# Copying position weights ahead of the transposes: one ScalarE copy, or four GpSimd copies by groups

## The chip, the cores and the metric

The kernel runs on one core of a Trainium2 chip. The metric is the device time of one execution in microseconds; lower is better. A core has five engines that run their own instruction streams: TensorE (PE in the profile, its weight loads PEld), VectorE (DVE), ScalarE (ACT), GpSimd (POOL) and SyncE (SP), which here only issues DMAs. Each engine takes its instructions in order; they wait for each other through semaphores.

## The reference

Two layers act on x of shape (2, 512, 64, 64) in float32. Layer 0, where the change lies, is a deformable convolution: for each pixel and each of 16 channel groups it predicts nine sampling offsets and a softmax mask, samples the projected image bilinearly, and projects the sum.

```python
xproj = inp @ in_w + in_b
x1 = gelu(layernorm(depthwise_conv3x3(x) + dw_b))
offset = x1 @ off_w + off_b
mask = softmax((x1 @ mask_w + mask_b).reshape(N, H, W, G, P), -1)
out = _dcnv3_core(xproj, offset, mask)   # 9 bilinear samples a group
out = out @ out_w + out_b
...
x = x + _L0(_gn(x), ...)                 # layer 0, group norm ahead
x = x + _L1(_gn(x), ...)                 # layer 1: attention over 4096 pixels, batch norm
```

## The kernel before

**Layer 0** takes about the first third of the time. The two images are cut into 16 chunks of 512 pixels (eight rows of 64), and each chunk passes four stages, all of them generators whose steps are interleaved by hand:

- project (line 758): normalise the rows on ScalarE (xn), multiply by in_w on TensorE (pq), copy out (xj, line 764) and store the image as pixel rows (xt) in HBM.
- features (from line 771): a 3x3 depthwise convolution as nine taps per channel block. The first is on ScalarE; eight are scalar_tensor_tensor on VectorE (line 788), each reading two SBUF tensors. GpSimd adds the blocks (tot, lines 794 and 796) for the layer norm's mean; Gelu follows.
- weights (from line 833): TensorE multiplies the features by the offset and mask weights (po, line 842), VectorE adds the bias (o, line 847). Since all offsets here are smaller than one pixel, the nine bilinear samples fall in a 5x5 window, so the stage builds, for each pixel and group, 25 position weights: aw of 128 pixels x 5 x 5 x 64, where the 64 are four pixel blocks times 16 groups. GpSimd clears aw (line 838), VectorE adds nine 3x3 products to it (lines 885 and 890). Then aw is rearranged into at, laid out as group, block, position (padded from 25 to 32); TensorE transposes it, four groups into one PSUM tile p_tr (line 901), and ScalarE copies each tile to awT (line 902).
- sample (from line 919): TensorE spreads awT over the pixels of small patches (pb, line 930), ScalarE copies that to bt (line 935), TensorE multiplies it with the image patches (pa, line 949), ScalarE copies to dT (line 961), TensorE applies out_w (py, line 970), and VectorE adds bias and x and takes statistics (lines 975 and 976).

The order on every engine is written out in the function period. In one period, sample works on chunk i, weights on chunk i+1, features and project further ahead. The copy from aw to at is the last step of weights within a period; its four transposes are the first steps of the next one. On ScalarE's queue the copies xj and dT of other stages stand behind it. In the first image's periods the statistics of the second image (pieces xraw, line 713) are slipped between VectorE's steps (image_stats).

The PSUM tiles pq, p_tr, po, py and the means share one tag with four buffers; at shares a buffer with tx of the same stage; aw has one buffer, so the next clearing of aw waits until the copy has read it.

**Layer 1** (from line 1112 on) is the attention. It touches nothing of the change.

Of the kernel before, what the change touches and what calls it, by code (L numbers as in the profile page):

```python
# [523 lines left out]
NW = 25  # L524
# [46 lines left out]
def window_path(ctx: ExitStack, tc: tile.TileContext, t_in: dict, out: bass.AP, far: bass.AP, sums: bass.AP):  # L571
    nc = tc.nc
# [57 lines left out]
    with ExitStack() as l0:  # L630
# [66 lines left out]
        def image_stats(n):  # L697

            mv = sm.tile([P, KB, 2], F32, name="gn_mv")
            size = CH if n == 0 else CH // 2  # L700
            pieces, ahead = deque((kb, h) for kb in range(KB) for h in range(S // size)), deque()
            for kb in range(KB):
                st = sm.tile([P, 16, 6], F32, name="gn_st")
                for h in range(S // size):
                    if n == 0:
                        t = img[kb][:, h * size : (h + 1) * size]
                    else:
                        while len(ahead) < 3 and pieces:
                            k2, h2 = pieces.popleft()
                            ahead.append(io.tile([P, size], F32, name="xraw", bufs=3))  # L710
                            nc.sync.dma_start(ahead[-1], x_v[n, :, k2, h2 * size : (h2 + 1) * size])
                        t = ahead.popleft()
                    nc.vector.bn_stats(st[:, h, :], t)
                    yield
                nc.vector.bn_aggr(mv[:, kb, :], st[:, : S // size].rearrange("p a b -> p (a b)"))
            yield
            result = []
            yield from group_norm_steps(mv, KB, sm, ps, result)
            sc, bi = result
            gn[n] = [sm.tile([P, KB], F32, name=f"gn_{k}{n}") for k in ("scale", "bias")]  # L720
            nc.vector.tensor_copy(gn[n][0], sc)
            nc.vector.tensor_copy(gn[n][1], bi)
# [110 lines left out]
        def weights(i):  # L833

            f = feats.pop(i)
            o = sm.tile([P, 3, NP, 4 * G], F32, name="o")
            aw = sm.tile([P, 5, 5, 4 * G], F32, name="aw")
            nc.gpsimd.memset(aw.rearrange("p y x q -> p (y x q)"), 0.0)
            for t in range(4):
                po = ps.tile([P, CH], F32, tag="mm", name="po")  # L840
                for kb in range(KB):
                    nc.tensor.matmul(  # L842
                        po[:, : 3 * GP], f[:, kb, t * P : (t + 1) * P], om_w[:, kb].rearrange("p a k g -> p (a k g)"),
                        start=(kb == 0), stop=(kb == KB - 1),
                    )
                yield
                nc.vector.tensor_add(
                    o[:, :, :, t * G : (t + 1) * G].rearrange("p a k g -> p (a k) g"),
                    po[:, : 3 * GP].rearrange("p (a g) -> p a g", g=G), om_b.rearrange("p a k g -> p (a k) g"),
                )  # L850
                yield

            m = o[:, 2]
            nc.scalar.activation(m, m, AF.Exp)
            yield

            tx = sm.tile([P, 2, 3, NP, 4 * G], F32, tag="tx", name="tx")
            for d, by in ((0, -1.0), (2, 1.0)):
                nc.vector.tensor_scalar(tx[:, :, d], o[:, 0:2], by, 0.0, ALU.mult, ALU.max)
            nc.vector.scalar_tensor_tensor(  # L860
                tx[:, :, 1].rearrange("p a k q -> p a (k q)"), tx[:, :, 0].rearrange("p a k q -> p a (k q)"), 1.0,
                tx[:, :, 2].rearrange("p a k q -> p a (k q)"), ALU.subtract, ALU.subtract, reverse0=True
            )
            yield

            nc.scalar.activation(o[:, 0:2], tx[:, :, 1], AF.Relu, scale=-1.0, accum_out=far[:, i : i + 1])
            yield
            sx = sm.tile([P, 4 * G], F32, name="sx")
            nc.vector.tensor_reduce(sx, m.rearrange("p k q -> p q k"), AX.X, ALU.add)
            rs = sm.tile([P, 4 * G], F32, name="rs")  # L870
            nc.vector.reciprocal(rs, sx)
            nc.gpsimd.tensor_add(sums[:, 0], sums[:, 0], sx)
            nc.gpsimd.tensor_add(sums[:, 1], sums[:, 1], rs)
            nc.vector.tensor_mul(m, m, rs.unsqueeze(1).to_broadcast([P, NP, 4 * G]))
            yield
            my = sm.tile([P, 3, NP, 4 * G], F32, name="my")
            nc.vector.tensor_mul(my, tx[:, 1], m.unsqueeze(1).to_broadcast([P, 3, NP, 4 * G]))
            yield
            myk = my.rearrange("p d k q -> p k d q")
            txk = tx[:, 0].rearrange("p d k q -> p k d q")  # L880
            for k in (4, 0, 1, 2, 3, 5, 6, 7, 8):
                kx, ky = divmod(k, 3)
                dst = aw[:, ky : ky + 3, kx : kx + 3, :]
                pk = dst if k == 4 else sm.tile([P, 3, 3, 4 * G], F32, tag="pk", name="pk")
                nc.vector.tensor_mul(  # L885
                    pk, myk[:, k].unsqueeze(2).to_broadcast([P, 3, 3, 4 * G]),
                    txk[:, k].unsqueeze(1).to_broadcast([P, 3, 3, 4 * G]),
                )
                if k != 4:
                    nc.vector.tensor_add(dst, dst, pk)  # L890
                yield
            at = sm.tile([P, G, 4, 32], F32, tag="tx", name="at")
            nc.scalar.copy(
                at.rearrange("p g t w -> p w t g")[:, :NW], aw.rearrange("p y x (t g) -> p (y x) t g", t=4)
            )
            yield

            for b in range(4):
                pt = ps.tile([P, 4, P], F32, tag="mm", name="p_tr")
                for g in range(4):  # L900
                    nc.tensor.transpose(pt[:, g, :], at[:, 4 * b + g].rearrange("p t w -> p (t w)"), ident)
                nc.scalar.copy(awT[:, 4 * b : 4 * b + 4, :], pt)  # L902
                yield
# [186 lines left out]

        run(image_stats(0), project(0), value_weights(), features(0), project(1))
        v = Chain(weights, 0)
        v(23)
        run(features(1), project(2), output_bias())
        fetch(0, 0)
        fetch(0, 1)
        later, y, f = image_stats(1), Chain(sample, NSEQ), Chain(features, 2)
        with tc.manual_schedule():
            f()
            for i in range(NSEQ):  # L1100
                if i == NCH - 3:
                    run(later)
                w, m, g = Chain(weights, i + 1), Chain(sample, i), Chain(features, i + 3)
                period(y, v, m, w, f, g, Chain(project, i + 3), lambda: next(later, None))
                y, v, f = m, w, g
            y.rest()
# [5 lines left out]
    with ExitStack() as l1, tc.manual_schedule():  # L1112
# [8 lines left out]
        with ExitStack() as at, ExitStack() as inner:  # L1121
            aw = at.enter_context(tc.tile_pool(name="w1w", bufs=1))
# [421 lines left out]
```

## Time and profile before

| | |
|---|---|
| median of 3 runs | 3732.9 us (3732.38 to 3734.91) |
| profiled execution | 3730.4 us, span 3728.5 us |
| PE / DVE / ACT / POOL busy | 92% / 63% / 35% / 8% of the span |
| copies from aw to at, ScalarE | 16, mean 2958 ns, 47.3 us in all, between 154 and 1236 us |
| p_tr transposes | 256, in 16 groups of 16 |
| awT copies, ScalarE | 64, mean 597 ns |
| aw clearings, GpSimd | 16, mean 1439 ns |
| GpSimd in all | 291.7 us busy |

The span runs from the first to the last instruction; the execution's own time is a little longer. A row of the profile names line, engine, operation, output and input by the program's names, with their shapes, then the busy time and the mean of one, then the idle time of that engine just ahead and what ended it. A line of the timeline begins with start and duration in us; neighbours of the same kind are merged, and the figure in square brackets is the idle time ahead with its releaser.

### The profile page before, as it was taken

What the parts mean: (1) busy time and instruction counts of PE and PEld (TensorE: products, weight loads), DVE (VectorE), ACT (ScalarE), POOL (GpSimd) and SP (SyncE); (2) the same over time, 40 slices, a digit from 0 to 9 for tenths busy, and PEclk for the clock granted to TensorE, in tenths of its full rate; (3) what the DMA queues carried; (4) which work ended last, traced back from release to release, by engine and by line L of the source; (5) the groups of instructions that cost most, each with busy time, mean ns of one, the idle gap of its engine ahead of it and who ended that gap; (6) DMA issues with size and microseconds to landing.
All of it is one profiled execution on the core that took longest, in us unless ns stands there. A gap on an engine that the chain in (4) does not pass through costs nothing.

```text
span 3728.5 us, 38957 instructions
## 1 busy us (share of the span) xinstructions
PE 3417.3 (92%) x15151; PEld 2434.0 (65%) x15151; DVE 2347.9 (63%) x3575; ACT 1300.0 (35%) x1691; POOL 291.7 (8%) x190
## 2 busy tenths in 40 slices
PE   4678889999998799999999999999999999999990
PEld 1345455555555577777777777777777777777770
DVE  5788888998996476545554554567455455545544
ACT  1466677787776331111111111122111121111114
POOL 2112111211211020000000000022000000000000
PEclk9799999999999899999999999999999999999995
DMA  7233443243332344343334334444433333343349
GB/s 238 61 99 106 124 119 117 89 121 118 105 116 70 101 194 172 102 158 131 128 115 150 129 107 144 141 156 159 165 110 111 131 128 113 108 148 116 115 157 391
DMA packets 180181, 500.06 MB, mean 134 GB/s; under 512 B 22640, under 2 KB 64368, under 8 KB 170512
## 3 DMA queue, kind: packets, MB, share of 16 engines
q1 hardware_dynamic: 176496, 473.34, 37.7%
q10 hardware_dynamic: 3456, 24.12, 1.7%
q8 instruction: 121, 1.98, 0.2%
q14 instruction: 76, 0.62, 0.0%
q0 software_dynamic: 32, 0.00, 0.0%
HBM read 406.09 MB, written 91.29 MB: 133 GB/s over the span
## 4 chain that ended last, share of the span: by engine, by line
PE 77%; DVE 13%; DMA 4%; ACT 2%; issue 2%; SPq 1%; POOL 1%; ACTq 0%; DVEq 0%; POOLq 0%
PE acc L1375 41%; DVE conv L788 7%; PE pS L1222 7%; PE p L1413 7%; PE py L970 5%; PE pq L758 5%; PE pa L949 4%; PE pv L1262 3%; PE pk L1316 1%; PE po L842 1%; DMA xraw<-in_x 1%; PE p_mean L801 1%; DVE aw L890 1%; DMA out<-ct 1%; DVE pk L885 1%
## 5 line engine op out<-in xcount | busy, mean ns | idle before, releaser
L1375 PE MATMUL acc<-e,v 128*128 128x256 f32 x3072 | 768.3, 386 | 0.0
L1375 PE MATMUL acc<-tt,v 128*128 128x256 f32 x3072 | 748.2, 380 | 0.5 <-DMA v<-wv 0.4
L1226 ACT ACTIVATE e<-pS 128x1024 f32<-128x1024 f32 x256 | 262.1, 1024 | 1386.5 <-PE pS L1222 1313.0
L1375 PEld LDWEIGHTS acc<-e,v 128*128 128x128 f32 x3072 | 566.6, 190 | 233.1 <-issue 165.3
L1375 PEld LDWEIGHTS acc<-tt,v 128*128 128x128 f32 x3072 | 582.4, 190 | 91.2 <-issue 10.6
L1229 DVE TENSOR_TENSOR t<-e 128x256 f32<-128x256 f32 x256 | 109.0, 426 | 761.7 <-ACT e L1226 761.7
L788 DVE SCALAR_TENSOR_TENSOR conv<-xn,L_conv_dw_w_sb,conv 128x504 f32<-128x504 f32 (+1 forms) x512 | 399.7, 795 | 31.8 <-ACT conv L783 19.4
L1239 DVE TENSOR_TENSOR tot<-tot,e 128x512 f32<-128x512 f32 x480 | 330.0, 688 | 8.3
L949 PEld LDWEIGHTS pa<-bt,patch 96*128 96x128 f32 x2048 | 250.8, 196 | 63.5 <-issue 36.9
L1222 PE MATMUL pS<-q,kq 64*128 64x512 f32 x1024 | 289.0, 641 | 0.0
L935 ACT COPY bt<-pb 96x1024 f32<-96x1024 f32 x124 | 232.9, 1989 | 93.4 <-PE pb L930 93.4
L949 PE MATMUL pa<-bt,patch 96*128 96x128 f32 x2048 | 254.6, 281 | 9.8 <-ACT dT L961 5.8
L970 PE MATMUL py<-dT,L_conv_out_w_sb 128*128 128x512 f32 x512 | 238.0, 610 | 7.4 <-ACT awT L902 7.4
L758 PE MATMUL pq<-L_conv_in_w_sb,xn 128*128 128x512 f32 x512 | 235.5, 604 | 4.0 <-ACT xn L748 4.0
L1413 PE MATMUL p<-t,v 128*128 128x256 f32 x1024 | 231.5, 382 | 1.8 <-DMA v<-wv 1.8
L1413 PEld LDWEIGHTS p<-t,v 128*128 128x128 f32 x1024 | 192.1, 190 | 48.5 <-issue 21.2
L961 ACT COPY dT<-pa 32x256 f32<-32x256 f32 x496 | 179.6, 362 | 76.2 <-PE pa L949 67.3
L842 PE MATMUL po<-om_w_pg,feat 128*128 128x432 f32 x512 | 202.7, 540 | 0.0
L970 PEld LDWEIGHTS py<-dT,L_conv_out_w_sb 128*128 128x128 f32 x512 | 97.9, 197 | 122.8 <-issue 111.4
L758 PEld LDWEIGHTS pq<-L_conv_in_w_sb,xn 128*128 128x128 f32 x512 | 94.0, 194 | 108.5 <-issue 93.1
L842 PEld LDWEIGHTS po<-om_w_pg,feat 128*128 128x128 f32 x512 | 92.8, 190 | 90.0 <-issue 88.4
L1222 PEld LDWEIGHTS pS<-q,kq 64*128 64x128 f32 x1024 | 77.1, 184 | 84.9 <-issue 84.9
(203 smaller groups left out, 3737.6 us busy)
## 6 DMA issues: line engine op xcount, KB each, us to landing
v<-wv SPq DMA_DIRECT2D x252, 768.0 KB
patch<-xt SPq DMA_DIRECT2D x256, 192.0 KB
v<-wv SPq DMA_DIRECT2D x256, 128.0 KB
wv<-v SPq DMA_DIRECT2D x32, 896.0 KB
xt<-xj SPq DMA_DIRECT2D x128, 128.0 KB
res<-in_x SPq DMA_DIRECT2D x64, 256.0 KB
wx<-res SPq DMA_DIRECT2D x64, 256.0 KB
xq<-wx SPq DMA_DIRECT2D x16, 1024.0 KB
```

The lines of the kernel that those rows point to most:

```text
L758: nc.tensor.matmul(pq, xn[:, kb, 1 + 2 * t : 3 + 2 * t, :].rearrange("p r c -> p (r c)"), in_w[:, kb, :], start=(kb == 0), stop=(kb == KB ...
L788: nc.vector.scalar_tensor_tensor(dst, src, wt, dst, ALU.mult, ALU.add)
L842: nc.tensor.matmul(po[:, : 3 * GP], f[:, kb, t * P : (t + 1) * P], om_w[:, kb].rearrange("p a k g -> p (a k g)"), start=(kb == 0), stop=(k ...
L935: copy(bt[:SN].rearrange("s g q d -> s d (g q)")[:, d0 : d0 + 4, :], pb[:SN])
L949: nc.tensor.matmul(pa[:, p], xp[:SN, p, cb * P : (cb + 1) * P], bt[:SN, 4 * cb : 4 * cb + 4, PX * s + p, :], start=True, stop=True,)
L961: copy(dst, src)
L970: nc.tensor.matmul(py, out_w[:, kb, cb * P : (cb + 1) * P], dT[:, kb, :], start=(kb == 0), stop=(kb == KB - 1))
L1222: nc.tensor.matmul(pS[:, h, :], kq[r, 2 * (kp // 4) + h, c0 : c0 + P], qs[qb][r, :], start=True, stop=True)
L1226: nc.scalar.activation(e.rearrange("p a q -> p (a q)"), pS.rearrange("p h q -> p (h q)"), AF.Exp)
L1239: nc.vector.tensor_add(tots[qb], tots[qb], e2[:, h, :])
L1375: nc.tensor.matmul(acc[j][:, cb * HQ : (cb + 1) * HQ], v[:, j, cb * P : (cb + 1) * P], ops[j], start=(kp + cb == 0), stop=(kp + cb == NPAI ...
L1413: nc.tensor.matmul(p7[:, cb * HQ : (cb + 1) * HQ], v7[:, cb * P : (cb + 1) * P], t3, start=(k + cb == 0), stop=(k + cb == NPAIR + 2),)
```

## The change

The copy from aw to at is issued on GpSimd instead of ScalarE, and in four instructions instead of one. Each copies four of the 16 groups (128 x 25 positions x 4 blocks x 4 groups, 400 elements a partition). The four transposes of a group of four come in the same order as before; each first one now waits for the part that holds its groups.

```diff
             at = sm.tile([P, G, 4, 32], F32, tag="tx", name="at")
-            nc.scalar.copy(
-                at.rearrange("p g t w -> p w t g")[:, :NW], aw.rearrange("p y x (t g) -> p (y x) t g", t=4)
-            )
+            for b in range(4):
+                gs = slice(4 * b, 4 * b + 4)
+                nc.gpsimd.tensor_copy(
+                    at.rearrange("p g t w -> p w t g")[:, :NW, :, gs],
+                    aw.rearrange("p y x (t g) -> p (y x) t g", t=4)[:, :, :, gs],
+                )
             yield
```

## The prediction

> **What bounds the kernel now.** I read the whole-kernel chain first, then the rows of the copy, then one period boundary in order of time, because the copy runs once per period (16 times, 154 to 1236 us).
>
> ```profile
> span 3728.5 us, 38957 instructions
> ...
> PE 77%; DVE 13%; DMA 4%; ACT 2%; issue 2%; SPq 1%; POOL 1%; ACTq 0%; DVEq 0%; POOLq 0%
> ```
>
> The kernel is bound by PE, with DVE behind it; ACT holds 2% of the chain. Who waits for the copy (its row, then "who waited for it"):
>
> ```profile
> L893 ACT COPY at<-aw x16: 2888/2966/3007, 154.5 to 1233.2; 128x1600 f32<-128x1600 f32 x16
> ...
>   PE p_tr L901: 35.3, 15
> ```
>
> PE does stop for it, 35.3 us over 15 boundaries, so at most about 1% is at stake. One boundary, from the timeline:
>
> ```profile
> 629.25 9.99 DVE L788 SCALAR_TENSOR_TENSOR conv<-xn,L_conv_dw_w_sb,conv 128x504 f32<-128x504 f32 x13
> ...
> 630.97 2.99 ACT L893 COPY at<-aw 128x1600 f32<-128x1600 f32 x1
> ...
> 634.01 1.97 PE L901 MATMUL p_tr<-ident,at 128*128 128x128 f32 x16 [1.83 <-ACT at L893]
> ...
> 636.42 3.70 PE L970 MATMUL py<-dT,L_conv_out_w_sb 128*128 128x512 f32 x8 [0.44 <-ACT awT L902]
> ...
> 640.16 0.75 DVE L975 SCALAR_TENSOR_TENSOR res<-py,L_conv_out_b_sb,res 128x512 f32<-128x512 f32 x1 [0.93 <-PE py L970]
> ...
> 644.32 0.61 DVE L847 TENSOR_TENSOR o<-po,om_b_pg 128x432 f32<-128x432 f32 x1 [2.68 <-PE po L842]
> ```
>
> The weights aw are complete at 629.33, but ACT is in other work until 630.97. PE waits 1.83 us for the copy, then 0.44 us for awT; awT, dT and xj all queued behind it on ACT. DVE runs 13 conv taps meanwhile and then has 0.93 + 2.68 = 3.6 us of slack before it needs PE's po. From there DVE sets the pace. So at this boundary PE's lateness is what counts, up to the 3.6 us.
>
> What GpSimd does to DVE shows in two places of the same timeline view:
>
> ```profile
> 150.38 3.39 POOL L814 TENSOR_TENSOR sq<-sq,feat 128x512 f32<-128x512 f32 x2
> 150.95 1.70 DVE L885 TENSOR_TENSOR pk<-my,tx 128x576 f32<-128x576 f32 x1
> 152.69 1.70 DVE L890 TENSOR_TENSOR aw<-aw,pk 128x576 f32<-128x576 f32 x1
> ```
>
> Here two GpSimd adds run beside two VectorE products. And four GpSimd copies beside a tiny product:
>
> ```profile
> 30.46 3.61 POOL L667 COPY om_w_pg<-om_w_sb 128x432 f32<-128x432 f32 x4 [26.39 <-DMA om_w_sb<-in_om_w]
> ```
>
> The product, in VectorE's own timeline of that time:
>
> ```profile
> 32.34 0.85 DVE L608 TENSOR_TENSOR gn_d<-gn_d 128x4 f32<-128x4 f32 x1
> ```
>
> DVE products of 0.76 us take 1.70 beside a GpSimd add: the two alternate, one instruction each. A copy with one input does it too: the 4-element product of 0.85 us takes 0.16 at 558.13, where no GpSimd read runs.
>
> [...] 1.70 against 0.76 above, while the 1.44 us memset at 634.02 leaves the taps at 0.74. [...] The trace's own copy steps 36 bytes and takes (3.61 - 0.95)/3 = 0.89 us from start to start for 432 elements[...]. [...]
>
> **The change, part by part.** It removes 16 copies of 2.97 us (47.3 us) from ACT and puts 64 of 128x400 on GpSimd. No DMA moves. PE's, DVE's and SyncE's orders are unchanged; each group of four transposes now waits for its own part. On GpSimd the copies stand ahead of the next memset of aw (L838) and sum tot (L794); the memset already waited for the old copy (366.1 us of idle), and tot's first sum starts at 647.3, over 10 us later, so nothing is late behind the copies.
>
> The price d of one part: scaling the strided copy, 0.89 x 400/432 = 0.83; I take **0.85 us**. Below, the memset's rate (1.44/1600 = 0.9 ns an element) gives 0.36. Above, the writes go 512 bytes apart. ACT pays 1.85 ns an element there (2.97/1600)[...]. I take 0.85 because a scattered write should cost no more than the scattered read.
>
> Under taps: an add of 1.27 us alone and a 0.76 us product alternate every 1.74 us (150.38 to 152.12), so 0.29 overlaps. A copy and a tap (0.74) then need 0.85 + 0.74 - 0.29 = 1.30 us; each tap, 0.78 from start to start, grows by 0.52.
>
> *Eight boundaries from 629 to 1111 us.* Copy 1 asks at about 629.5, [...]ends at 630.7; copy 4 ends 3 x 1.30 later, 634.6. PE is free at 632.18 and has done three groups by then; the fourth takes 0.5, so py starts at 635.2 instead of 636.42, 1.2 us earlier. dT and xj leave ACT's queue earlier still. DVE pays 4 x 0.52 = 2.1: its taps, res and statistics, without the 0.93 wait, end at 641.64 - 0.93 + 2.1 = 642.8, before po (644.32 - 1.2 = 643.1). Were the slack gone, the 2.1 would be the loss. Sum: **-9.6**.
>
> *The last two (1174, 1233 us).* No taps run, and the chain itself passes through the copy:
>
> ```profile
> 1174.59 2.90 ACT at L893
> ...
> 1177.53 3.68 PE p_tr L901 x16
> ```
>
> From aw's end (1174.50) to 1181.21 it is 6.7 us. With parts: 0.1 + 0.85, then four groups of 0.92 at this slow PE rate: 4.6. Gain 2.1 each: **-4.2**.
>
> *Four early ones (237 to 480 us).* Here o follows DVE's statistics with no wait, so DVE sets the pace. Between aw and the first tap DVE waits for an image piece (xraw): 4.1, 2.8, 2.8 and 2.2 us. Copies of 0.85 take 3.4: nothing lost in the first; the fourth copy delays a tap by 0.6 in the next two, and the last loses 0.9. Sum **+2.1**.
>
> *At 556 us* the copy holds ACT while DVE waits for a square root behind it (3.67 us of idle). Two tiny products wait for copies, about 0.6 each: net **-0.8**. *At 154 us* ACT's rstd and later awT come earlier, but PE's input projection (to 170.5) sets the pace: **-0.6**.
>
> Sum -9.6 - 4.2 + 2.1 - 0.8 - 0.6 = **-13.1 us**. The profiled execution, 3730.4 us (span 3728.5 and 1.9 around it), becomes 3717.3; it lies 2.5 below the median of the three runs, 3732.9, which becomes 3719.8.
>
> **Rivals.**
>
> *Break-even (27%).* d of 1.0 to 1.25. At 1.25 the cycle is 1.70, copy 4 ends at 636.2 and py starts at 636.8, 0.4 late; DVE's +3.7 eats its slack. Eight times that, some 6 us more at the early boundaries, less 1.2 at the last two, gives about +7; d = 1.12 is zero. Time near 3732. For it: the scattered writes; against: the strided copy at 0.89.
>
> *Slower (18%).* The copies themselves become the wait before the transposes: place, line 901; price, 4d plus the taps between; it decides from d = 1.28. At 1.5 each of the eight loses 1.2 to 1.4 us (10), the early four 8 together, the last two nothing: +18, 3751. For it: ACT pays 1.85 ns an element in this copy against 1.16 in a plain one (0.595 us for 512, line 764). Against: the 0.89 us.
>
> *No interference (10%).* Copies slip between taps at no cost. PE is then free-running from 632.2: py at 634.2, 2.2 earlier, 17.6 over eight; with 4.2 and 1.4 it is -23, 3710. The 0.85 us product speaks against it.
>
> That the copy was hidden anyway is excluded by the 35.3 us of PE idle.
>
> **How the numbers follow.** The case worked out above has 45%, with its own range of 3714 to 3726 (d from 0.75 to 0.97); the rivals have 27, 18 and 10%. About 0.2% (7.5 us) is what a measurement can tell from no change. Faster: nearly all of the 45 and the 10, 0.53; within: 0.28; slower: 0.19. The range is 3708 to 3743: it takes in the no-interference case and the slower one up to d = 1.35, and leaves out about 15%.
>
> **What would show it.** Right: parts spaced 0.8 to 0.9 us where DVE is idle and about 1.3 under taps; four taps of about 1.3 at each boundary; PE's wait at line 901 down from 35.3 to about 20 us; py about 1.2 earlier after aw; the two last boundaries 2 shorter. Wrong: copies over 1.1 us; o at the eight boundaries waiting for DVE's statistics instead of po; or the early boundaries, where SyncE's queue follows DVE, losing several us each because late image pieces delay the patch loads.

## The result, and the profile after

The changed kernel takes 3711.8 us (median of 4 runs, 3709.6 to 3714.1) against 3732.6 us: a ratio of 0.9944, 95% interval 0.9927 to 0.9962, which is 14 to 27 us less. The forecast was 3719.8 us in a range of 3708 to 3743, with faster as the likelier side. The way and the range were right; the gain is half as large again as the 13 us of the sum, and the time lies just below the 3714 to 3726 of the case that was worked out. A later set of five runs read 3713.0 against 3731.7, ratio 0.9949 (0.9935 to 0.9963), 18.7 us.

The page of the changed kernel, its head and its chain:

```profile
span 3711.9 us, 39076 instructions
...
PE 76%; DVE 14%; DMA 5%; ACT 3%; issue 1%; SPq 1%; POOL 1%; ACTq 0%; POOLq 0%; DVEq 0%
```

The span is 16.6 us shorter, and the kernel is still bound by PE. The copies, in the view of the tile at (row, then who waited):

```profile
L895 POOL COPY at<-aw x64: 857/1257/1333, 154.4 to 1218.1; 128x400 f32<-128x400 f32 x64
...
  PE p_tr L904: 14.7, 11
```

PE's wait for the copy falls from 35.3 to 14.7 us. One boundary of the eight, from the timeline (start, duration, engine; lines behind the copy are 3 higher than before):

```profile
692.27 11.36 DVE L788 SCALAR_TENSOR_TENSOR conv<-xn,L_conv_dw_w_sb,conv 128x504 f32<-128x504 f32 x13
692.48 4.64 POOL L895 COPY at<-aw 128x400 f32<-128x400 f32 x4 [21.00 <-DVE aw L890]
...
695.28 0.59 ACT L764 COPY xj<-pq 128x512 f32<-128x512 f32 x1 [1.22 <-PE pq L758]
695.77 1.48 ACT L964 COPY dT<-pa 32x256 f32<-32x256 f32 x4
...
697.18 0.66 PE L904 MATMUL p_tr<-ident,at 128*128 128x128 f32 x4 [0.46 <-POOL at L895]
...
697.27 2.05 ACT L905 COPY awT<-p_tr 128x512 f32<-128x512 f32 x4
...
697.91 3.70 PE L973 MATMUL py<-dT,L_conv_out_w_sb 128*128 128x512 f32 x8
...
705.81 0.61 DVE L847 TENSOR_TENSOR o<-po,om_b_pg 128x432 f32<-128x432 f32 x1 [0.80 <-PE po L842]
```

The weights aw are complete at 692.35. py starts 5.56 us later; before it was 7.04 to 7.09. Two waits end together there: the last transposes end at 697.84, and the first awT copy, behind xj and dT on ScalarE, at 697.87. (py does not read awT. It needs one of the four PSUM buffers of the shared tag, and gets the one that this copy has emptied.) VectorE still waits for po, 0.80 us now. So each of these boundaries gave about 1.5 us: the period from aw to aw was 68.16 and is 66.68.

GpSimd's copies and VectorE's taps do take turns. The taps from aw to res, as groups of VectorE in that stretch, before and after:

```profile
L788 DVE SCALAR_TENSOR_TENSOR conv<-xn,L_conv_dw_w_sb,conv 128x504 f32<-128x504 f32 (+1 forms) x13 | 9.6, 745 | 0.4
```

```profile
L788 DVE SCALAR_TENSOR_TENSOR conv<-xn,L_conv_dw_w_sb,conv 128x504 f32<-128x504 f32 (+1 forms) x13 | 11.0, 850 | 0.4
```

Thirteen taps pay 1.4 us for four copies, out of the 3.6 us of slack. Where VectorE only waits for an image piece, the copies run freely:

```profile
395.25 3.10 POOL L895 COPY at<-aw 128x400 f32<-128x400 f32 x4 [23.90 <-DVE aw L890]
```

That is (3.10 - 0.90)/3 = 0.73 us from copy to copy there, and (4.64 - 1.27)/3 = 1.12 under taps.

| from aw complete to aw complete, by the two traces | before | after | difference |
|---|---|---|---|
| five periods, 154 to 556 us | 401.26 | 398.21 | -3.1 |
| the period from 556 to 629 us | 73.69 | 73.16 | -0.5 |
| eight periods, 629 to 1174 us | 545.17 | 533.27 | -11.9 |
| the last period, 1174 to 1233 us | 58.64 | 56.79 | -1.9 |
| last boundary, aw to py | 6.46 | 4.54 | -1.9 |

These rows make 19.3 us; the spans differ by 16.6, and what lies after them took 2.7 longer, within the 4.5 us over which this kernel's four runs spread. In the second set's trace the first row is 400.82, a difference of 0.4 only; the eight periods again make 533.29.

At the last two boundaries no taps run, and the chain passes through one part and then through the transposes, which start 1.0 us after aw (1158.95) instead of 3.0:

```profile
1159.08 0.87 POOL at L895
...
1160.00 3.67 PE p_tr L904 x16
```

### The profile page after: what moved, and what is told of

It reads as the page before. It is cut to its first block, busy times and chain, and to the rows that moved or that the text cites. A ratio compares the mean times of both kernels' runs of the same rounds, so it can differ in the third digit from the quotient of the medians.

```text
span 3711.9 us, 39076 instructions
## 1 busy us (share of the span) xinstructions
PE 3418.9 (92%) x15151; PEld 2434.2 (66%) x15151; DVE 2360.9 (64%) x3575; ACT 1257.8 (34%) x1675; POOL 353.4 (10%) x254
## 4 chain that ended last, share of the span: by engine, by line
PE 76%; DVE 14%; DMA 5%; ACT 3%; issue 1%; SPq 1%; POOL 1%; ACTq 0%; POOLq 0%; DVEq 0%
PE acc L1378 41%; DVE conv L788 7%; PE pS L1225 7%; PE p L1416 6%; PE py L973 5%; PE pq L758 4%; PE pa L952 4%; PE pv L1265 3%; DMA xraw<-in_x 1%; PE po L842 1%; PE pk L1319 1%; PE p_mean L801 1%; DVE aw L890 1%; DMA out<-ct 1%; DVE pk L885 1%
## 5 line engine op out<-in xcount | busy, mean ns | idle before, releaser
L788 DVE SCALAR_TENSOR_TENSOR conv<-xn,L_conv_dw_w_sb,conv 128x504 f32<-128x504 f32 (+1 forms) x512 | 411.1, 817 | 31.8 <-ACT conv L783 19.4
L1165 POOL TENSOR_TENSOR xsa<-xt 128x1024 f32<-128x1024 f32 x7 | 16.5, 2357 | 1261.4 <-ACT xt L1187 1261.4
```

What stands on the lines that cost most here:

```text
L788: nc.vector.scalar_tensor_tensor(dst, src, wt, dst, ALU.mult, ALU.add)
```

## Experiments

Two theories stood for the gain. In the queue theory, it counts that the copy leaves ScalarE, where xj, dT and awT stood behind it. In the parts theory, it counts that the first transposes can start when a quarter is copied.

**The engine alone.** One GpSimd copy of all 1600 elements. The edit, against the changed kernel:

```diff
-            for b in range(4):
-                gs = slice(4 * b, 4 * b + 4)
-                nc.gpsimd.tensor_copy(... [:, :NW, :, gs], ... [:, :, :, gs])
+            nc.gpsimd.tensor_copy(... [:, :NW], ...)
```

> GpSimd copies all 1600 elements in one instruction; the engine is moved, the cutting is not made. Queue theory (the gain comes from ScalarE's queue: xj, dT and awT no longer stand behind the copy): at 0.73 us for 400 elements one copy takes about 2.7 us, is done some 3.3 us after aw, and py still starts about 5.6 us after aw at the eight boundaries, as in the changed kernel (7.05 before); only the last two boundaries lose 1.7 us each against the changed kernel. Time 3714 to 3718. Parts theory (the gain comes from transposes that start on the first quarter): transposes start after the whole copy, py about 6.5 or later, time 3725 or more.

Measured: 3714.0 us against 3731.1, ratio 0.9955 (0.9939 to 0.9972). One boundary of its timeline:

```profile
690.41 3.32 POOL L893 COPY at<-aw 128x1600 f32<-128x1600 f32 x1 [21.00 <-DVE aw L890]
...
693.78 1.97 PE L901 MATMUL p_tr<-ident,at 128*128 128x128 f32 x16 [0.65 <-POOL at L893]
...
695.20 2.05 ACT L902 COPY awT<-p_tr 128x512 f32<-128x512 f32 x4
695.84 3.70 PE L970 MATMUL py<-dT,L_conv_out_w_sb 128*128 128x512 f32 x8
...
703.90 0.59 DVE L847 TENSOR_TENSOR o<-po,om_b_pg 128x432 f32<-128x432 f32 x1
```

py again starts 5.56 us after aw (690.28), and the period is 66.80 us: at the eight boundaries the engine alone makes nearly all of the gain. Only o has no wait left here, because the 13 taps last 12.40 us beside one long copy and 11.36 beside four short ones. (The long copy holds back a single tap, which takes 3.15 us; the 14 taps from 690.4 to 704.5 us average 916 ns, against 745 before.) At the last two boundaries py starts 6.53 and 6.39 after aw, as before the change (6.50 and 6.46): there the engine alone gains nothing.

**The parts alone.** nc.scalar.copy in place of nc.gpsimd.tensor_copy, four parts kept.

> ScalarE copies in four parts; the cutting is made, the engine is not changed. Queue theory: parts of about 0.9 us start 1.6 us after aw and end 5.1 after it, xj, dT and awT follow, py starts 7.1 to 7.4 us after aw at the eight boundaries, no gain there and none at the early ones; the last two gain 2 us each. Time 3727 to 3734. Parts theory: the first transposes start about 2 us earlier and py with them; time 3714 to 3720.

Measured: 3730.2 us, ratio 0.9996 (0.9987 to 1.0005). py starts 7.06 to 7.16 us after aw at the eight boundaries, although the first transposes start 2 us earlier than before, at 2.69. The list of waits (us, times, longest) shows where the time went:

```profile
PE py L973 <- ACT awT L905: 19.4, 15, 2.5
...
PE p_tr L904 <- ACT at L895: 10.4, 2, 6.3
```

PE's wait for the copy falls from 35.3 to 10.4 us, but py's wait for awT grows from 7.4 to 19.4. The parts theory falls for the eight. At the last two py starts 5.20 and 5.23 us after aw, 1.3 and 1.2 earlier than before; with the parts on GpSimd it is 4.51 and 4.54. So there the parts are needed, and most of their gain comes on either engine. In this trace the last period was no shorter for it (59.41 us, against 58.64).

**ScalarE held.** The changed kernel, plus a useless copy of dead data at the old place on ScalarE:

```diff
+            held = my.rearrange("p d k q -> p (d k q)")[:, :1344].rearrange("p (a b) -> p b a", b=32)
+            nc.scalar.copy(held, held)
```

> The changed kernel, with ScalarE given a useless copy of about 3 us (1344 strided elements of the dead tile my, onto itself) at the place where its copy to at stood; the result is not touched. Queue theory: py at the eight boundaries goes back to about 7 us after aw, and the early boundaries lose their gain of about 3 us; the last two keep theirs. Time 3726 to 3732. Parts theory, in which the transposes decide: nothing but awT is late, time 3712 to 3718.

Measured: 3728.1 us, ratio 0.9991 (0.9983 to 1.0). From its timeline:

```profile
700.93 2.86 ACT L900 COPY my<-my 128x1344 f32<-128x1344 f32 x1
...
704.42 0.63 PE L906 MATMUL p_tr<-ident,at 128*128 128x128 f32 x4 [0.58 <-ACT xj L764]
...
705.65 2.05 ACT L907 COPY awT<-p_tr 128x512 f32<-128x512 f32 x4
706.29 1.98 PE L975 MATMUL py<-dT,L_conv_out_w_sb 128*128 128x512 f32 x4 [1.25 <-ACT awT L907]
```

With four GpSimd copies in place and all transposes done by 705.05, py waits 1.25 us for awT. The period is 68.06 us, as before the change. This and the two runs above settle the eight boundaries: the gain comes from the 3 us that ScalarE no longer spends on the copy. It is 1.5 us and not 3, because xj then waits 1.22 us for pq, as the line of 695.28 above shows.

**Each part copied twice.** The price of GpSimd's work, doubled.

```diff
+                for _ in range(2):
                     nc.gpsimd.tensor_copy(
```

> The changed kernel, with each part copied twice on GpSimd, which doubles the price of a part. If GpSimd's copies and VectorE's taps take turns (1.13 us from copy to copy under taps, 0.73 without): eight copies end about 9.2 us after aw, py starts near 9.9 (5.6 in the changed kernel), so each of the eight boundaries loses 4.3, the last two 2.1 each and the early four 1.5 to 2.5 each: about 3755. If copies and taps did not take turns: eight copies end 6.0 after aw, py near 6.8, time about 3725.

Measured: 3765.8 us, ratio 1.0095 (1.0078 to 1.0112), 11 us above what the turn-taking case gave. py starts 10.16 us after aw, near the 9.9 of that case and far from 6.8. The period grew by 6 us instead of 4.3, and the timeline shows more time lost:

```profile
702.61 1.11 PE L905 MATMUL p_tr<-ident,at 128*128 128x128 f32 x4 [1.57 <-POOL at L896]
...
703.52 6.15 PE L974 MATMUL py<-dT,L_conv_out_w_sb 128*128 128x512 f32 x8
```

Behind three waits of about 1.5 us PE is slow: the same eight py matmuls take 6.15 us instead of 3.70. The TensorE clock that the trace shows as granted is 0.63 of full speed from 702 to 711 us, and 1.00 from 711 to 720; in the changed kernel it is 1.00 over the whole period from 692 to 759 us. At the early boundaries, where 1.5 to 2.5 us each were expected to be lost, the doubled copies cost nothing in sum (396.5 us from 153 to 550, against 398.2 in the changed kernel). The list of waits says why, VectorE's wait for image pieces before, then with doubled copies (us, times, longest):

```profile
DVE gn_st L713 <- DMA xraw<-in_x: 37.2, 8, 8.3
```

```profile
DVE gn_st L713 <- DMA xraw<-in_x: 19.7, 7, 4.8
```

At the four boundaries from 235 to 473 us o starts 1.0 to 5.7 us later after aw than before the change, and yet these periods together are no longer: what VectorE loses there comes off this wait.

**The early boundaries alone.** GpSimd's parts for the first six chunks, ScalarE's copy for the rest.

```diff
+            if i <= 5:
+                ...   # the four GpSimd copies
+            else:
+                nc.scalar.copy(...)
```

> The changed kernel's four GpSimd copies for the first six chunks only (up to the boundary at 556 us); later chunks keep ScalarE's one copy. The prediction's step said that these boundaries together cost 0.7 us (+2.1 - 0.8 - 0.6): time 0 to 1 above the kernel before. The trace of the changed kernel reads as a gain of about 3 us up to there, because VectorE's next wait for an image piece absorbs what GpSimd takes from it and SyncE's loads go out earlier: time 2 to 4 below the kernel before.

Measured: 3727.9 us against 3732.3, ratio 0.9990 (0.9983 to 0.9996): 1.5 to 6.3 us less. The prediction's +0.7 lies outside.

The traces of the other runs, one of each, say where this comes from when they are read together. SyncE's patch loads stand behind the stores of xt, which wait for xj on ScalarE:

| us | before | four parts on ScalarE | ScalarE held | this run | changed, two traces | one GpSimd copy |
|---|---|---|---|---|---|---|
| first patch load, after the aw at about 317 us | 6.33 | 6.38 | 6.31 | 5.24 | 5.23, 5.24 | 5.23 |
| the same at about 476 us | 5.74 | 5.78 | 5.62 | 4.64 | 4.61, 4.59 | 4.61 |
| the six early periods together (154 to 629 us before) | 475.0 | 477.5 | 479.1 | 473.4 | 471.4, 473.9 | 471.7 |

Where ScalarE keeps about 3 us of copying, the loads go out late and the six periods take 475 us or more, even with the four copies on GpSimd. Where ScalarE is free, the loads go out 1.1 us earlier and the periods take less than 474.

**The exchange of two steps at a period's end**, so that ScalarE does dT in the 1.2 us in which it waits for pq, and SyncE the patch loads ahead of the last store of xt.

```diff
             w(3)
+            m()
             p()
             more()
-            m()
```

> The changed kernel, with two steps at the end of each period exchanged, so that ScalarE does dT before the last xj, in the 1.2 us in which it waits. In the changed kernel the last transpose ends 5.49 us after aw and the awT copy behind dT at about 5.5, so both would have to move. If so: py stays at 5.5, time as the changed kernel, 3709 to 3714. If ScalarE's queue alone sets py: 0.6 us less at each of eight boundaries, 3705 to 3708.

Measured: 3701.1 us, ratio 0.9916 (0.9903 to 0.9930), more than either case had. py starts at 5.31 us instead of 5.56, only 0.25 earlier (66.34 us a period), 2.8 us over eight. The transposes hold py there: the last ones end at 5.5 as before, and py's first matmul overlaps them a little, while the first awT copy is done at 4.2. Most of the rest is ahead of these periods, which the same edit on the kernel before shows by itself:

> The kernel before, with only the exchange of the two steps (dT ahead of the last xj), ScalarE's one copy of 1600 elements kept. If the exchange gains by itself, about as in the changed kernel (10 us there): 3720 to 3724. If it only pays once the copy has left ScalarE: py still waits for awT behind the copy, 0.4 to 0.6 us at each of eight boundaries at most, 3726 to 3732.

Measured: 3722.8 us against 3731.7, ratio 0.9976 (0.9965 to 0.9986). The eight periods stay at 68.17 us, so py gains nothing while the copy is on ScalarE; the five periods from 151 to 546 us take 394.5 instead of 401.3. SyncE's and VectorE's timelines there, before:

```profile
403.61 5.67 SPq L914 DMA_DIRECT2D patch<-xt  x8
```

```profile
419.40 0.43 DVE L713 BATCH_NORM_STATS2 gn_st<-xraw 128x6 f32<-128x256 f32 x1 [8.30 <-DMA xraw<-in_x]
```

and with the exchange:

```profile
395.27 5.66 SPq L914 DMA_DIRECT2D patch<-xt  x8
```

```profile
409.21 0.43 DVE L713 BATCH_NORM_STATS2 gn_st<-xraw 128x6 f32<-128x256 f32 x1 [2.53 <-DMA xraw<-in_x]
```

The patch loads go out 3.4 us after aw (391.88) instead of 7.7 (395.87), and VectorE's longest wait for an image piece in this period is 2.5 us instead of 8.3. So SyncE's queue has a part in the pace of the early periods.

**The first part on VectorE.**

```diff
-                nc.gpsimd.tensor_copy(
+                (nc.gpsimd if b else nc.vector).tensor_copy(
```

> The changed kernel, with the first of the four parts copied by VectorE and three by GpSimd. The last part is there about 1.1 us earlier, transposes end 4.7 us after aw, but awT still stands behind dT on ScalarE: py stays near 5.5 at the eight boundaries and only the last two gain, 0.4 us each: 3708 to 3713. If GpSimd's last part alone sets py: 0.6 to 0.8 less at each of eight, 3704 to 3707.

Measured: 3710.0 us, ratio 0.9943 (0.9929 to 0.9956). Transposes end 4.60 us after aw, but py still starts at 5.56: awT is behind dT.

**Both edits.**

> Both of the last two edits. If the two waits end together in the changed kernel, only this one moves py, to about 4.8 us after aw, and VectorE's 0.8 us of slack before o is used up: 0.5 to 0.8 us less at each of eight boundaries and 0.4 at the last two, 3703 to 3708. If something else holds py, 3709 to 3714.

Measured: 3704.7 us, ratio 0.9926 (0.9912 to 0.9939). Now py starts at 4.44, as only both waits together allow, and o at 12.68 instead of 13.46. Five of the eight periods take 65.9 us, two 67.6 and one 66.7. In the two of 67.6 (620 to 687.6 and 753.5 to 821 us) the mean granted clock is 0.97, in the one between them 1.00, which fits the difference (0.03 of 67 us is about 2); what lowered the clock stays open. The time is no better than with the exchange alone.

**The changed kernel once more.**

> The changed kernel again, beside the next run on the same chip. The prediction's sum is 13 us below the kernel before, the four earlier runs read 21 below; its own profile is 17 below. Expected 3711 to 3716 where the kernel before reads 3732.

Measured: the 3713.0 us given with the result. The lowest median of all versions is that of the changed kernel with the exchange, 3701.1 us.

## Why the prediction was right or wrong, point by point

- *PE is late at the boundary because of the copy on ScalarE, 35.3 us in all*: right in kind, but the wait that counts was misread. With ScalarE held, py is late again (6.9 to 7.0 us after aw) although all copies are done by 4.9: what it waits for then is awT, behind ScalarE's queue. With parts on ScalarE the wait for the copy falls to 10.4 us and nothing is gained. So the 35.3 us did not measure what the copy cost.
- *Copies and taps take turns*: right in kind. The no-interference rival came nearer to the time (3710) but for a wrong reason: taps grow from 745 to 850 ns on average, and doubling the copies costs 54 us, though part of that is the lower clock. The range of 3708 to 3743 held because it took in this rival; that the time fell inside it owes something to luck.
- *The price d, 0.85 us, and 1.30 us in turn with a tap*: too high. 0.73 alone and 1.12 under taps; the four taps that meet a copy last 1.08 to 1.11 us, not 1.3. With its scattered write the copy still cost less than the one with a 36-byte read step, from which the estimate was scaled (1.8 ns an element, against 2.1). The rivals of break-even and slower, which needed d of 1.0 and more, fall with it.
- *Eight boundaries, -1.2 us each, -9.6*: measured 1.49 each, -11.9, since d was smaller. One clause was wrong: that dT and xj would be out of the way "earlier still". ScalarE's chain of xj, dT and awT ends at 697.87, in the same moment as the transposes, and a single GpSimd copy gives the same py.
- *The last two, -4.2*: measured 1.9 + 1.9 = 3.8. Here the parts theory holds.
- *Four early ones, +2.1, with -0.8 at 556 us and -0.6 at 154 us, +0.7 in all*: the step that failed. It took VectorE to set the pace because o follows its statistics with no wait. Up to o this holds, only the loss was put too high: o starts 0.06 to 0.37 us later after aw at the four boundaries, 0.7 us in sum instead of 2.1, since four copies of 0.73 us nearly fit into VectorE's wait for the image piece. But later in the same period VectorE waits up to 8.3 us for another piece, and that piece stands on SyncE behind stores that wait for xj, which ScalarE's copy had delayed (around 396 us the last two stores of xt began 4.0 us after aw before the change, at 399.90, and 2.9 us after it with the change, at 398.06). Measured for these boundaries alone: -4.4 (-1.5 to -6.3). In the table of the early periods the gain goes with a free ScalarE. Its size for a single execution stays loose: the two traces of the changed kernel differ by 2.5 us over these six periods.
- *The range to 3743 and 0.53 for faster*: wide because the estimate of d was open from 0.75 to above 1.28. The strided copy at hand in the trace bounded it better than that.

## What to carry to other kernels

When a copy moves to an idle engine, look first at what stood behind it on the old one: here that queue, not the copy's own speed or its cutting, made most of the gain (3714.0 us with one GpSimd copy, 3730.2 with four parts on ScalarE, against 3711.8 with both). Cutting paid where the consumer was otherwise idle, at the last two boundaries (py 4.51 and 4.54 us after aw, against 6.53 and 6.39 with one copy), and it cost VectorE less here (1.4 us for thirteen taps, against 2.4 with one copy). Before charging lost time on an engine that sets the pace at one place, look for its next wait: here a wait for a load later in the period took the loss (37.2 us in all before, 19.7 with doubled copies), and the load itself came earlier through stores that ScalarE had held up (around 396 us the last two of them began 4.0 us after aw before the change, 2.9 with it).

## What was not expected of the hardware

- A GpSimd copy of 400 elements that reads runs of four and writes 512 bytes apart takes 0.73 us from copy to copy, less for each element (1.8 ns) than one that reads 36 bytes apart and writes in order (0.89 us for 432, 2.1 ns).
- One GpSimd copy of 1600 elements takes 2.9 us alone, no more than ScalarE's 2.96 us.
- With doubled copies the granted clock was 0.63 of full speed from 702 to 711 us, behind three waits of PE of 1.5 to 1.6 us, and eight py matmuls took 6.15 us instead of 3.70. At the last boundaries, behind a longer wait (4.16 us in the changed kernel), sixteen transposes take 3.6 to 3.7 us before and after the change, against 1.97; the granted clock there is 0.50 (1160 to 1164 us). That the waits lower the clock is not shown by a run of its own.
